# Selective-scan kernel: the order of softplus and side steps around a scan unit's B

## The chip, the cores and the metric

The kernel runs on one core of one Trainium2 chip, as one program. The metric is the device time of that core in microseconds (us); lower is better. The core has five engines that each work through their own instructions in order: TensorE (PE in the profile; PEld is its weight load), VectorE (DVE), ScalarE (ACT), GpSimd (POOL) and SyncE (SP, which here only issues DMA transfers).

## The reference

Four layers of a two-dimensional selective scan, each added to its input after a group norm. The sizes are a batch of 8, images of 48 x 48 (L = 2304 positions), 96 channels, 192 inner channels (Din), 16 states (N), 4 scan directions (K). The layers differ in small ways; layer 0 stands for them:

```python
xz = einsum('bhwc,ec->bhwe', x, in_proj_w);  xc, z = split(xz, 2, axis=-1)
xc = silu(depthwise_conv3x3(xc) + conv_b)
xs = stack([x0, x1, x0[..., ::-1], x1[..., ::-1]], axis=1)   # rows, columns, both ways
x_dbl = einsum('bkdl,kcd->bkcl', xs, x_proj_weight)
dts, Bs, Cs = split(x_dbl, [R, R + N], axis=2)
dts = einsum('bkrl,kdr->bkdl', dts, dt_projs_weight)
A = -exp(A_logs)
delta = softplus(dts + dt_projs_bias)
def step(h, inp):                       # along the L positions
    u, dl, Bv, Cv = inp
    dA = exp(dl[..., None] * A)
    h = h * dA + (dl * u)[..., None] * Bv[:, :, None, :]
    y = einsum('bkdn,bkn->bkd', h, Cv)
    return (h, y)
# ys + xs * Ds, the four directions summed, layer norm, * silu(z), out projection
```

For each channel and state there is one recurrence over the positions: h = h * dA + delta * u * B, and the output is the sum of h * C over the 16 states.

## The kernel before, in words

**Tiling.** Two images at a time make a pair (4 pairs a layer). The 192 channels of two images make three tiles `t` of 128 partitions. With two phases `ph` (row order or column order) and two directions `d` there are 12 groups for each layer and pair, and the 2304 positions of a group are cut into 3 chunks of 768. A chunk has 16 units `n`. One unit is one tensor of 128 partitions x 768 positions: two states of 64 channels each (`states`). A unit takes one scan instruction, so layers 0 to 2 have 3 layers x 4 pairs x 12 groups x 3 chunks x 16 = 6912 units. Layer 3 takes another, shorter path (class `Edge`, `l in short`), which the diff leaves as it is. Below, a block means the 16 units of one chunk.

**What one unit needs.** For unit n:

- B: the state's B row spread over 64 partitions. For ten units of a block, TensorE makes it in PSUM by four matmuls with the matrix `pick` (`spread`, L678); VectorE then multiplies it by delta * u (L810). For the six units n = 2, 5, 7, 10, 13, 15 (`pooled`) B comes from DRAM instead, by two DMAs from `xd` into `bb` (L740), and GpSimd makes the product with delta * u (`weigh`, L757). Then the PSUM buffer is used for the unit's decay.
- The decay exp(delta * a): one ScalarE activation (L780), into SBUF `da` or, for pooled units, into the PSUM buffer `b`.
- The scan, on VectorE (L814), and the product with C on GpSimd (`cb`, L823). C too is spread by DMA (L740).
- The sum over the states: TensorE adds the product into the PSUM accumulator `acc` (`add_up`, L870), two units later (`LAG = 2`).
- The last value of h is kept for the next chunk by a small ScalarE copy, the carry (`catch_up`, L698).

The PSUM pool of these buffers has two (`pb`, bufs=2): the B or decay of unit k + 1 takes the buffer of unit k - 1, which the scan of k - 1 frees.

**Softplus of the coming chunk.** `prepare` is a generator that makes delta and delta * u of the next chunk while the present one is scanned, in 15 steps; each `step(coming)` runs it to its next yield, one for each unit, beginning at n = 15 of the chunk before. For each half of 384 positions: the dt matmul (L614), then Abs, Relu and Exp on ScalarE (L622 to L624), then Ln, Identity and Identity (L626 to L628), then two steps of sums on TensorE, the first of `e` and `w1`, the second of `lg` and `x` (L634), then four copies to `dl` (L589), the product with u on VectorE (L642, L645), and four copies to `du`. In the text S1 to S15 are these steps: S1 at n = 15, S2 at n = 0, S3 at n = 1, first sums S4 at n = 2, second sums S5 at n = 3, S7 at n = 5, second half S8 at n = 6 to S15 at n = 13, its sums at n = 9 and 10.

**Side steps.** The work before a pair's scans (`prologue`: group norm, in projection L411 and L420, convolution L314, x projection L472) and after them (`epilogue`: L1031 to L1123) are generators as well. `side_step` advances one of them by one step. A step may issue work on any engine, DMAs on SP too.

**The order.** The instruction order of each engine is that of the Python loop in `run`, kept by `keep_order`. For unit k the loop issues: `collected()` (the copy of a finished accumulator, L887, when there is one), `get_ready(k + 1)` (loads for units k + 4 and k + 5, then B or decay of unit k + 1, then `weigh` and `decay` of unit k + 3), `catch_up()`, `scan(n)`, `add_up` of unit k - 2, and then `beside()`: one softplus step and one side step. At n = 3, where an accumulator was copied (`busy`), `beside()` stands ahead of `add_up`; at n = 2 (`ends`) there is no side step. So before, both kinds of step follow the B of unit k + 1 in the same pass.

Of the kernel before, what the change touches and what calls it, by code (L numbers as in the profile page):

```python
# [103 lines left out]
def ss2d_layers_kernel(ctx: ExitStack, tc: tile.TileContext, x_in, consts, weights, out):  # L104
# [470 lines left out]
    def load_dt(c):  # L575
        r = layers[c.l].rank
        c.dts = sm1.tile([64, SCAN], F32, name="dts", tag="dts")
        for b in c.batches:
            q0 = 32 * b if c.t == 2 else 0
            nc.sync.dma_start(  # L580
                c.dts[q0 : q0 + r, : c.m],
                state[c.l, c.p]["xd"][c.ph, b, c.d * r : (c.d + 1) * r, c.c0 : c.c0 + c.m],
            )
# [101 lines left out]
    def store_some(n):  # L685
        for _ in range(min(n, len(late_stores))):
            o, z, at = late_stores.pop(0)
            nc.sync.dma_start(o[:, at], z[:, at])

    def collected():  # L690
        some = bool(late_sums)
        while late_sums:
            late_sums.pop(0)()
        return some

    def catch_up():
        while late_act:
            nc.scalar.copy(*late_act.pop(0))  # L698
# [450 lines left out]
    def drain(g):  # L1149
        for _ in g:  # L1150
            pass

    def step(g):
        next(g, None)
# [7 lines left out]
    def side_step(*sides):  # L1162

        for s in sorted(sides, key=lambda s: (not s.held, s.made / s.total)):
            got = next(s.g, s)
            s.held = got is True
            if got is not s and got is not GATED:
                s.made += 1
                return True
        return False  # L1170
# [3 lines left out]
    def mark():  # L1174
        marks.append(len(tc._region_blocks()[0].instructions))
# [12 lines left out]
    LAG = 2  # L1188
    LOADS, DECAYS = 3, 2

    def run(pairs, short):


        def units():
            for l, p in pairs:
                for gi, (t, ph, d) in enumerate(groups):
                    if l in short:
                        c = Edge(l, p, t, ph, d)
                        for i in range(NS // QUAD):
                            yield (l, p, gi * (NS // QUAD) + i), c, i  # L1200
                        continue
                    group = {}
                    for i in range(len(SCANS)):
                        c = Chunk(l, p, t, ph, d, i, group, c if d == 1 and i == 0 else None)
                        for n in range(NS):
                            yield (l, p, (gi * len(SCANS) + i) * NS + n), c, n

        def begin(l, p, first=False):
            if l not in layers:
                layers[l] = Layer(l)  # L1210
            return prologue(l, p, l in short, first)

        todo = list(units())

        def rest_of_sum(k):
            before = todo[k - 1][1] if k > 0 else None
            if isinstance(before, Chunk) and (k == len(todo) or todo[k][1] is not before):
                before.add_up(NS)

        def get_ready(k):  # L1220

            def early(ahead, what):
                for i in range(0 if k == 0 else k + ahead, min(k + ahead + 1, len(todo))):
                    getattr(todo[i][1], what)(todo[i][2])

            early(LOADS + 1, "load_b")
            early(LOADS, "load")
            if k == 0:
                todo[0][1].decay(todo[0][2])
            if k < len(todo):  # L1230
                (l, p, _), c, n = todo[k]
                if n == 0 and c.first and l not in short:
                    c.group["carry"] = capool.tile([P, NS], F32, name="carry", tag="carry")
                c.spread(n)
            early(DECAYS, "weigh")
            for i in range(k + DECAYS if k else 1, min(k + DECAYS + 1, len(todo))):
                todo[i][1].decay(todo[i][2])

        rest = begin(*pairs[0], first=True)
        while next(rest) is not READY:  # L1240
            pass
        rest = Side(rest)
        chunks = list(dict.fromkeys(c for _, c, _ in todo))
        drain(prepare(chunks[0]))
        behind = ahead = Side()
        coming = iter(())
        done = None
        mark()
        get_ready(0)
        for k, ((l, p, unit), c, n) in enumerate(todo):  # L1250
            at = pairs.index((l, p))
            following = pairs[at + 1] if at + 1 < len(pairs) else None
            if l in short and unit == 0:
                mark()
            per = NS // QUAD if l in short else NS
            all_units = len(groups) * (per if l in short else len(SCANS) * per)
            place["tiles"] = 3 * unit // all_units
            store_some(1)
            if done:
                behind, done = Side(epilogue(*done), 199), None  # L1260
            if unit == LAG and following:
                ahead = Side(begin(*following), 311)
            if k == 0:
                coming_to = 1
                coming = prepare(chunks[coming_to])
            if n == max(0, per - 1 - DECAYS):
                while coming_to < len(chunks) and not chunks[coming_to].ready:
                    next(coming)
            if n == 10 and coming_to + 1 < len(chunks):
                z = chunks[coming_to + 1]  # L1270
                if (z.l, z.p) == (l, p):
                    load_dt(z)
            busy = collected()
            get_ready(k + 1)
            catch_up()
            c.scan(n)
            if n == per - 1:
                drain(coming)
                if unit + 1 + per == all_units:
                    drain(behind.g)  # L1280
                    drain(ahead.g)
                coming_to = chunks.index(c) + 2
                coming = prepare(chunks[coming_to]) if coming_to < len(chunks) else iter(())


            def beside():
                step(coming)

                for _ in range(10 if l in short else 0 if ends else 1):
                    side_step(rest) or side_step(behind, ahead)  # L1290

            ends = l not in short and k > LAG and todo[k - LAG][2] == 0
            if busy and l not in short:
                beside()
            if k >= LAG:
                (bl, bp, _), b, bn = todo[k - LAG]
                rest_of_sum(k - LAG)
                if bl in short:
                    collected()
                b.add_up(bn)  # L1300
                if k > LAG and todo[k - LAG - 1][0][:2] != (bl, bp):
                    done = todo[k - LAG - 1][0][:2]
            if not (busy and l not in short):
                beside()
        for i in range(len(todo) - LAG, len(todo)):
            collected()
            rest_of_sum(i)
            todo[i][1].add_up(todo[i][2])
            catch_up()
        collected()  # L1310
        rest_of_sum(len(todo))
        collected()
        drain(epilogue(*pairs[-1]))

    last = NLAYER - 1
    run([(l, p) for l in range(NLAYER) for p in range(NPAIR)], (last,))

    keep_order(*marks[:2])
# [8 lines left out]
    with tc.If(nc.values_load(again, min_val=0, max_val=1) > 0):  # L1327
        run([(last, p) for p in range(NPAIR)], ())
# [95 lines left out]
```

## Time and profile before

| | |
|---|---|
| median of 3 runs | 20188.83 us (20176.15 to 20194.05) |
| the profiled execution | 20200.44 us |
| its span, first to last instruction | 20198.6 us |
| mean granted TensorE clock | 0.908 |
| units of layers 0 to 2 (first scan's start to last scan's end) | 178 to 18298 us |
| DMA | 4200.80 MB, mean 208 GB/s |

In the lines of the page's groups, the parts are: line, engine, operation, tile written and tiles read with their shapes, count; then busy time in us and mean ns of one; then the idle time of the engine just before these instructions, and what ended most of it. A line of waits reads: engine and line that waited, what it waited for, total us, times, longest. A line of the timeline reads: start in us, duration, engine, line, operation, tiles, count. A line of windows reads: the stretch in us, its length, then the busy time and the number of instructions of PE, PEld, DVE, ACT and POOL, then the granted TensorE clock, the share of DMA time, GB/s. The busy time of TensorE is modelled, and its matmuls overlap.

### The profile page before, as it was taken

How to read it: one execution, taken by the hardware profiler on the slowest of the kernel's cores; microseconds unless marked ns; L12 is line 12 of the kernel's file. 1: busy time of each engine (PE TensorE's matmuls, PEld its weight loads, DVE VectorE, ACT ScalarE, POOL GpSimd, SP SyncE). 2: the span in 40 equal slices, each digit the busy share in tenths (PEclk: the TensorE clock that was granted, in tenths of full speed). 3: DMA queues.
4: the chain of work that ended last, by engine and by line, in shares of the span. 5: the costliest groups of instructions: out<-in, count | busy, mean ns of one | idle time of the engine just before them, and what ended most of it. 6: DMA issues, size and time to landing. Idle time of an engine off the chain costs nothing.

```text
span 20198.6 us, 314848 instructions
## 1 busy us (share of the span) xinstructions
PE 16790.8 (83%) x92962; PEld 7792.6 (39%) x92962; DVE 17667.0 (87%) x14161; ACT 16224.6 (80%) x30014; POOL 17769.4 (88%) x10121
## 2 busy tenths in 40 slices
PE   7888887887888888888887888888888887888886
PEld 3333333333333333333333333333333333334565
DVE  6999998998999999999999999999999999996553
ACT  6777887887887887887887887877877887887786
POOL 6999999999999999999999999999999999995442
PEclk9998998998998998998998999998999998999997
DMA  5888888888888888888888888888888888884221
GB/s 157 231 224 223 226 222 221 227 223 220 225 226 224 224 231 224 223 228 223 225 228 223 223 225 226 223 226 221 221 224 222 222 225 221 220 222 117 79 74 50
DMA packets 2021150, 4200.80 MB, mean 208 GB/s; under 512 B 375920, under 2 KB 789360, under 8 KB 2017904
## 3 DMA queue, kind: packets, MB, share of 16 engines
q1 hardware_dynamic: 2019440, 4180.55, 79.2%
q8 instruction: 762, 12.48, 0.3%
q14 instruction: 948, 7.77, 0.2%
HBM read 4026.64 MB, written 152.27 MB: 207 GB/s over the span
## 4 chain that ended last, share of the span: by engine, by line
PE 21%; ACT 17%; DVE 14%; DMA 10%; issue 9%; POOL 3%; SPq 2%; DVEq 0%; POOLq 0%; ACTq 0%
DVE da L814 7%; PE acc L870 5%; PE ps L634 4%; DMA bb<-xd 4%; DVE b L810 4%; DMA cb<-xd 4%; ACT b L780 3%; ACT dl L589 3%; PE ps L314 2%; PE b L678 2%; ACT du L589 2%; POOL cb L823 2%; DVE bb L814 2%; ACT da L780 2%; SPq L740 1%
## 5 line engine op out<-in xcount | busy, mean ns | idle before, releaser
L823 POOL TENSOR_TENSOR cb<-cb,da 128x768 f32<-128x768 f32 x4320 | 7835.9, 1819 | 749.3 <-issue 253.1
L870 PE MATMUL acc<-cb,twin 128*64 128x384 f32 x27648 | 7200.8, 539 | 721.3 <-POOL cb L823 704.5
L814 DVE TENSOR_TENSOR_SCAN da<-da,carry,b 128x768 f32<-128x768 f32 x2880 | 5223.2, 1814 | 176.0 <-DVE b L810 0.9
L757 POOL TENSOR_TENSOR bb<-bb,du 128x768 f32<-128x768 f32 x2592 | 4716.9, 1820 | 222.2 <-DMA bb<-xd 125.6
L823 POOL TENSOR_TENSOR cb<-cb,bb 128x768 f32<-128x768 f32 x2592 | 4706.8, 1816 | 100.2 <-DVE bb L814 50.7
L810 DVE TENSOR_TENSOR b<-du,b 128x768 f32<-128x768 f32 x4320 | 4085.6, 946 | 690.2 <-PE b L678 604.2
L678 PE MATMUL b<-brow,pick 96*64 96x512 bf16 (+2 forms) x18816 | 2852.5, 353 | 1886.2 <-DVE da L814 1528.4
L780 ACT ACTIVATE da<-dl,a 128x768 f32<-128x768 f32 x4320 | 4011.3, 930 | 213.5 <-POOL cb L823 183.0
L870 PEld LDWEIGHTS acc<-cb,twin 128*64 128x64 f32 x27648 | 2452.5, 149 | 2998.4 <-POOL cb L823 1333.5
L814 DVE TENSOR_TENSOR_SCAN bb<-b,carry,bb 128x768 f32<-128x768 f32 x1728 | 3109.6, 1800 | 106.0 <-ACT b L780 35.6
L780 ACT ACTIVATE b<-dl,a 128x768 f32<-128x768 f32 x2592 | 2335.3, 901 | 623.2 <-DVE da L814 598.4
L678 PEld LDWEIGHTS <-pick 96*64 96x64 bf16 x18816 | 1077.9, 115 | 4164.4 <-DVE da L814 2717.6
L814 DVE TENSOR_TENSOR_SCAN da<-da,b 128x768 f32<-128x768 f32 x1440 | 2525.3, 1754 | 87.4 <-DVE b L810 1.4
L314 PE MATMUL ps<-pad,diag 128*64 128x480 f32 (+1 forms) x8640 | 2339.7, 567 | 34.6 <-ACT du L589 24.4
L589 ACT COPY dl<-ps 64x384 f32<-64x384 f32 x3456 | 1632.6, 472 | 697.9 <-PE ps L634 659.6
L589 ACT COPY du<-ps 64x384 f32<-64x384 f32 x3456 | 1633.5, 473 | 200.7 <-DVE ps L645 109.8
L634 PE MATMUL ps<-du,cst 128*64 128x384 f32 (+1 forms) x7296 | 1704.5, 506 | 76.5 <-ACT du L628 65.6
L814 DVE TENSOR_TENSOR_SCAN bb<-b,bb 128x768 f32<-128x768 f32 x864 | 1502.1, 1739 | 145.5 <-ACT b L780 92.2
L634 PE MATMUL ps<-dl,cst 128*64 128x384 f32 (+1 forms) x7296 | 1485.2, 483 | 0.0
L614 PE MATMUL ps<-dts,w 6*128 6x384 f32 (+5 forms) x2432 | 961.4, 605 | 205.0 <-DMA dts<-xd 105.4
L622 ACT ACTIVATE du<-ps,w 128x384 f32<-128x384 f32 (+1 forms) x912 | 519.9, 570 | 714.6 <-PE ps L614 701.0
L314 PEld LDWEIGHTS ps<-pad,diag 128*64 128x64 f32 x8640 | 751.8, 139 | 885.0 <-issue 729.6
(144 smaller groups left out, 19166.4 us busy)
## 6 DMA issues: line engine op xcount, KB each, us to landing
cb<-xd SPq DMA_DIRECT2D x13952, 192.0 KB
bb<-xd SPq DMA_DIRECT2D x5184, 192.0 KB
brow<-xb SPq DMA_DIRECT2D x864, 72.0 KB
ey<-yd SPq DMA_DIRECT2D x256, 216.0 KB
cb<-xd SPq DMA_DIRECT2D x128, 384.0 KB
yd<-y SPq DMA_DIRECT2D x216, 192.0 KB
ex<-xs SPq DMA_DIRECT2D x256, 108.0 KB
xb<-parts SPq DMA_DIRECT2D x96, 216.0 KB
```

Source lines behind the costliest of these rows:

```text
L314: nc.tensor.matmul(ps[half, :m], ly.diag[:, int(t == 2), j, half], pad[:, r0 + dy : r0 + dy + nr, dx : dx + W], start=(j == 0), stop=(j == 8),
L589: nc.scalar.copy(z[64 * h : 64 * h + 64, g, at], v[64 * g : 64 * g + 64])
L614: nc.tensor.matmul(o[:, :m], ly.dtw[q0 : q0 + r, k, chans], dts[q0 : q0 + r, at], start=True, stop=True,)
L622: nc.scalar.activation(e, v, AF.Abs, bias=bias)
L634: nc.tensor.matmul(v[half], ident[:, half], z1, start=(i == 0), stop=(i == 3))
L678: nc.tensor.matmul(o[64 * h : 64 * h + 64], pick[:, b, n : n + 1].to_broadcast([2 * NR, 64]), rows, start=True, stop=True,)
L757: nc.gpsimd.tensor_mul(b, b, self.du[n % 2])
L780: nc.scalar.activation(da, self.dl[n % 2], AF.Exp, scale=layers[self.l].a2[:, int(self.t == 2), n % 2, k, i : i + 1],)
L810: nc.vector.tensor_mul(b, self.du[n % 2], b)
L814: nc.vector.tensor_tensor_scan(way(h), way(da), way(b), start, ALU.mult, ALU.add)
L823: nc.gpsimd.tensor_mul(c, c, h)
L870: nc.tensor.matmul(self.acc[64 * g : 64 * g + 64, a, : self.m // 2], twin, c[:, a, :], start=False, stop=(pair + 2 == NS and not self.turns),)
```

## The change

For pooled units of layers 0 to 2 (`ahead_of_b`), the softplus step and the side step are issued ahead of `get_ready(k + 1)`, so ahead of the next unit's B, and no `beside()` follows. At n = 15 the side step goes ahead; the first step of the next `prepare` goes right after the old one is drained, ahead of `add_up`. Units 3, 9 and 10 (`full`) have no side step any more. Units 1, 12 and 14 (`free`), whose next unit is pooled, have a second one, ahead of `add_up`. A block has 15 side steps before and after.

```diff
+    full, free = (3, 9, 10), (1, 12, 14)
...
+            def aside():
+                side_step(rest) or side_step(behind, ahead)
+
             busy = collected()
+            ends = l not in short and k > LAG and todo[k - LAG][2] == 0
+
+            ahead_of_b = l not in short and c.pooled(n)
+            if ahead_of_b:
+                if n < per - 1:
+                    step(coming)
+                if not ends and n not in full:
+                    aside()
             get_ready(k + 1)
             catch_up()
             c.scan(n)
@@
                 coming = prepare(chunks[coming_to]) if coming_to < len(chunks) else iter(())
 
+                if ahead_of_b:
+                    step(coming)
 
             def beside():
                 step(coming)
 
-                for _ in range(10 if l in short else 0 if ends else 1):
-                    side_step(rest) or side_step(behind, ahead)
-
-            ends = l not in short and k > LAG and todo[k - LAG][2] == 0
+                for _ in range(10 if l in short else 0 if ends or n in full else 1):
+                    aside()
+
+            if l not in short and n in free:
+                aside()
             if busy and l not in short:
                 beside()
...
-            if not (busy and l not in short):
+            if not (busy and l not in short) and not ahead_of_b:
                 beside()
```

## The prediction, made before the changed kernel ran

> **What bounds the kernel now.** I read the page's engine lines first, then its costliest groups, then the list of waits, then one block of 16 units in the timeline.
>
> ```profile
> PE 16790.8 (83%) x92962; PEld 7792.6 (39%) x92962; DVE 17667.0 (87%) x14161; ACT 16224.6 (80%) x30014; POOL 17769.4 (88%) x10121
> ...
> L823 POOL TENSOR_TENSOR cb<-cb,da 128x768 f32<-128x768 f32 x4320 | 7835.9, 1819 | 749.3 <-issue 253.1
> ...
> L814 DVE TENSOR_TENSOR_SCAN da<-da,carry,b 128x768 f32<-128x768 f32 x2880 | 5223.2, 1814 | 176.0 <-DVE b L810 0.9
> ...
> L810 DVE TENSOR_TENSOR b<-du,b 128x768 f32<-128x768 f32 x4320 | 4085.6, 946 | 690.2 <-PE b L678 604.2
> ```
>
> No engine is full. The units of layers 0 to 2 run from 178 to 18298 us: 432 blocks (6912 scans / 16) of 41.95 us each. In that stretch VectorE is busy 16756.6 us (38.8 a block), GpSimd 17055.7 (39.5). By the instruction records, GpSimd starts a unit's product 0.4 to 2.5 us after its scan ended and is back near the low end after units 1, 6, 9 and 14: it follows, VectorE leads. So **a block lasts as long as VectorE's work plus VectorE's waits** (3.2 us), and I price the change there.
>
> ```profile
> PEld L678 <- DVE da L814: 2717.6, 1691, 6.7
> PE b L678 <- DVE da L814: 1528.4, 1125, 6.1
> ...
> ACT dl L589 <- PE ps L634: 659.6, 411, 4.7
> DVE b L810 <- PE b L678: 604.2, 623, 10.5
> ...
> PEld ps L634 <- ACT du L628: 138.8, 166, 4.4
> ```
>
> Columns: total us, times, longest. TensorE stands at the next B (L678) until the scan two units earlier frees its PSUM buffer, mostly ahead of B(0), B(14) and B(8) (1.3, 1.1 and 0.5 us a block, sorted by unit). Yet VectorE waits for B elsewhere: at unit 1 (0.58 us a block), 11 (0.39), 6 and 12 (0.12 each). The last line matters below: the softplus sums wait for ScalarE's L628. One block (scan(0) begins at 10654.17), five answers: two of clock and busy time by window, then ScalarE, TensorE and VectorE.
>
> ```profile
> 10650.00:10655.00 5.00, 3.31 (x14) 0.97 (x16) 4.96 (x4) 2.44 (x6) 4.98 (x4) 0.76 1.03 239
> 10655.00:10660.00 5.00, 5.00 (x20) 2.20 (x22) 4.89 (x4) 4.91 (x10) 5.00 (x4) 0.56 1.00 241
> ```
> ```profile
> 10656.37 0.91 ACT L780 ACTIVATE b<-dl,a 128x768 f32<-128x768 f32 x1
> 10657.20 0.93 ACT L780 ACTIVATE da<-dl,a 128x768 f32<-128x768 f32 x1
> 10658.02 0.18 ACT L698 COPY carry<-da 128x1 f32<-128x1 f32 x1
> 10658.10 0.62 ACT L626 ACTIVATE dl<-du,ones 128x384 f32<-128x384 f32 x1
> 10658.62 0.60 ACT L627 ACTIVATE du<-du,ones 128x384 f32<-128x384 f32 x1
> 10659.26 0.62 ACT L628 ACTIVATE du<-du,ones 128x384 f32<-128x384 f32 x1
> ```
> ```profile
> 10658.82 0.85 PE L678 MATMUL b<-brow,pick 96*64 96x512 bf16 x4
> 10659.43 0.88 PE L870 MATMUL acc<-cb,twin 128*64 128x384 f32 x4
> 10660.08 1.52 PE L634 MATMUL ps<-du,cst 128*64 128x384 f32 x8
> ```
> ```profile
> 10658.68 1.79 DVE L814 TENSOR_TENSOR_SCAN bb<-b,carry,bb 128x768 f32<-128x768 f32 x1
> 10660.39 0.94 DVE L810 TENSOR_TENSOR b<-du,b 128x768 f32<-128x768 f32 x1
> ```
>
> TensorE's clock (0.76, 0.56) falls where it had stood before B(0). B(3) is made at 10658.82, well ahead of mul(3) at 10660.39; the sums come after it, at 10660.08, just after L628 ends at 10659.88. The change turns these two round.
>
> **What the Trainium skill says.** "TensorE: Matmul & The Clock Gate", Part 1: TensorE falls to half clock after an idle window of about 3.4 us and returns after a busy one. The trace agrees: 579 half-clock stretches, the shortest 3.4 us; in the blocks 18% of the time is at half clock, but 66% of unit 0's and 1% of that of units 4 and 5. Mul(1) waits 1.00 us where the clock is half and 0.05 where it is full. The same page's table says the queues of ScalarE, VectorE and GpSimd are strict FIFO; so here, what stands behind a waiting instruction waits too, and on TensorE as well the matmuls behind L870 stand while it waits 704.5 us for GpSimd.
>
> **The change part by part** (us a block, to be multiplied by 432).
>
> Counts: 15 side steps before and after; softplus step order unchanged. No operation is added or removed.
>
> 1. *Side steps at 14 (two) and ahead of B(0) at 15.* TensorE stands 1.77 us ahead of B(0); two more side steps there cost about 0.7 each (0.81 for a convolution step's four matmuls, none for a pure ScalarE step), so they fit. What stood between B(0) and B(1) shrinks from sum(13), L614 and a side step to sum(13) and L614, and the clock should stay up. Of the 0.58 at mul(1), about 0.25 are 27 blocks where L614 waits some 4 us for a late dt row (pair boundaries); those stay. **Gain 0.33** (0.1 to 0.45). B(0) had 1.0 of slack: cost 0; without that slack, each microsecond lands on mul(0).
>
> 2. *First sums ahead of B(3), at unit 2.* The longest new wait. TensorE cannot pass the sums before L628. Over all blocks L628 ends 3.48 after the exponential of b(2) starts, fixed within 0.05; that one needs the end of scan(0) (its PSUM buffer) and now starts 0.83 after it. With L614 ahead of sum(13), I take 0.35. Add the side step now ahead of L626 at unit 1 (estimate 0.2 of ScalarE: its 34.1 busy us a block less exponentials, softplus and copies leaves 2 to 3 for 15 side steps), the four matmuls left after L628 (half of eight in 1.3: 0.65), B(3) (0.05 + 0.55). Mul(3) can start 0.35 + 3.48 + 0.2 + 0.65 + 0.6 = 5.3 after scan(0). VectorE is there at 5.22 (measured) - 0.33 = 4.9. Wait 0.4; with scatter **loss 0.5** (0.2 to 0.9). Queued behind B(3): sum(16), B(4), the second sums; none is late, since B(4) has 1.2 of slack and VectorE moves later with it.
>
> 3. *Units 9 and 10: side steps out, second sums of half two ahead of B(11).* Sum(7) waits for GpSimd's product 7; the first sums start 0.24 after it, then a side step, then B(11). The side step (mean 0.43 between sums and B) becomes 1.3 of sums. Replacing one by the other in each block raises the wait from 0.39 to 0.80; blocks that had an L472 side step there (about as long as the sums) show 0.73, those with L314 0.27. I take **loss 0.3** (0 to 0.5). B(12) then has only sum(8) ahead: **gain 0.12**.
>
> 4. *Unit 5, 7, 13: softplus step and side step ahead of B(6), B(8), B(14).* S7, S9, S15 are ScalarE's, nothing on TensorE. A side step ahead of B(8) uses the 0.5 it stands; B(14) has 1.75 of slack: 0. B(6)'s 0.12 wait and the 0.22 of scan(10) for its exponential shrink: **gain 0.1** (0 to 0.2).
>
> 5. *Side steps closer together.* An epilogue's VectorE product (L1086, L1108; 32 a pair, 0.9 a block) follows ScalarE's step at once. Before, a scan always lay between; now none does at the second steps of 1, 12, 14 nor at 5, 7, 13, 15: 7 of 15 places, each 0.3 to 1.5 us of VectorE standing. 0.9 x 7/15 x 0.7 = 0.3, a part behind waits 2 and 3: **loss 0.1** (0 to 0.3).
>
> 6. *DMAs and GpSimd's own side work.* On SP the side steps' transfers now stand ahead of the cb and bb loads of their unit; one waiting for its copy holds these. Loads run 3 to 4 units (8 to 10 us) ahead, and GpSimd's longest group waits only 125.6 us in the run for bb: 0. Without that cover the delay would show at L757. GpSimd's products of the prologue only change places: 0. The unrolled last layer (18298 to the end) is untouched.
>
> Sum: -0.33 + 0.5 + 0.3 - 0.12 - 0.1 + 0.1 = +0.35 a block, x 432 = +151 us. The profiled execution took 20200.4 (span 20198.6 and 1.8 around), 11.6 over the median 20188.8. 20200.4 + 151 - 12 = **20340**.
>
> **The rivals.**
>
> - *Main case, slower:* mul(3)'s wait takes the place of mul(1)'s and mul(11)'s grows: 20340, own range 20240 to 20480. For: L628's time is fixed. Against: part 2 turns on 0.4 us. Chance 0.42.
> - *Faster: the clock stays up.* The two longest stands of TensorE are filled, half clock goes nearly everywhere; parts 1, 3b and 4 give 0.55, units 0 and 8 (waits 0.45 and 0.35 when cold, 42% and 24% of blocks) another 0.15; loss 2 only 0.2, 3 and 5 nothing: -0.5 x 432 = -216, 19973. It decides if mul(3) waits under 0.2 and mul(11) no more than now. For: 1.00 against 0.05 at mul(1). Against: the mean wait of VectorE for B is only 604 us in all. Chance 0.36.
> - *The two cancel,* 20190: waits 2 and 3 at 0.3 and 0.15. Chance 0.10.
> - *Clearly slower:* 2, 3 and 5 at their upper ends: 0.9 + 0.5 + 0.3 - 0.55 = +1.15, +497, about 20685. Chance 0.12.
> - That the change does not take effect is out: in the order of the built programs L634 stands ahead of L678 at unit 2 and a side step ahead of B(0).
>
> **How the numbers follow.** Faster 0.36, slower 0.42 + 0.12 = 0.54, within 0.2% (40 us, about what a measurement of this kernel can tell from no change; its runs lie within 18 us) 0.10. The range leaves out about a tenth at each end: from 19880, past the faster rival by as much as its own terms may be off (0.2 a block, 90 us), to 20680, just short of the worst.
>
> **What would show it.** Right: the wait of L810 for L678 at unit 1 falls under 0.3 us a block and one of about 0.5 appears at unit 3; "PE ps L634 <- ACT du L628" grows several times over; L678's wait for L814 falls by over a third; the mean clock rises above 0.93. Wrong: mul(3) starts with its scan as now, or the wait at mul(11) does not grow; then the faster case holds.

## The result, and the profile after

The changed kernel takes 20951.75 us (median of 5 runs, 20949.28 to 20959.5) against 20194.05 us for the kernel before (5 runs beside it): ratio 1.0378, 95% interval 1.0363 to 1.0392. It is **slower by 758 us**, or 1.75 us for each of the 432 blocks. The forecast was slower as well, but by 151 us; the measured time lies above the whole range (to 20680).

The page of the changed kernel: the span and the engines, then the groups that answer to those shown of before.

```profile
span 20949.9 us, 315270 instructions
...
PE 16850.4 (80%) x92962; PEld 7727.8 (37%) x92962; DVE 17722.3 (85%) x14161; ACT 16191.4 (77%) x30014; POOL 17790.5 (85%) x10121
...
L823 POOL TENSOR_TENSOR cb<-cb,da 128x768 f32<-128x768 f32 x4320 | 7833.6, 1817 | 1442.9 <-issue 388.5
...
L814 DVE TENSOR_TENSOR_SCAN da<-da,carry,b 128x768 f32<-128x768 f32 x2880 | 5223.8, 1814 | 174.6 <-ACT b L780 1.8
L810 DVE TENSOR_TENSOR b<-du,b 128x768 f32<-128x768 f32 x4320 | 4091.1, 947 | 1237.7 <-PE b L678 1007.8
```

No instruction was added, and the large groups take as long as before (1817, 1814 and 947 ns each, before 1819, 1814 and 946). What grew is idle time: ahead of VectorE's product with B (L810) from 690.2 to 1237.7 us, ahead of GpSimd's product (L823) from 749.3 to 1442.9. The list of waits says who made VectorE wait (columns: total us, times, longest us).

```profile
PEld L678 <- DVE da L814: 1713.7, 1087, 5.0
...
DVE b L810 <- PE b L678: 1007.8, 835, 11.2
PE b L678 <- DVE da L814: 983.9, 721, 4.3
...
PEld ps L634 <- ACT du L628: 594.0, 412, 8.0
...
PE ps L634 <- ACT du L628: 335.3, 264, 7.3
...
ACT dl L589 <- PE ps L634: 226.6, 230, 3.5
DVE b L810 <- PE acc L870: 221.2, 197, 5.5
PEld ps L1031 <- ACT ey L1074: 209.1, 102, 4.3
DVE eyc L1108 <- ACT ps L270: 185.5, 92, 7.4
```

The lines of before for these waits that are not shown yet (the first of them is for experiment e10):

```profile
DVE bb L814 <- ACT b L780: 127.8, 75, 5.2
...
PEld ps L1031 <- ACT ey L1074: 89.2, 77, 3.0
...
DVE eyc L1108 <- ACT ps L270: 85.4, 73, 7.4
...
DVE b L810 <- PE acc L870: 76.0, 59, 4.8
...
PE ps L634 <- ACT du L628: 65.6, 53, 3.1
```

TensorE stands less ahead of B (1713.7 and 983.9 us where it was 2717.6 and 1528.4), as the change arranges, and ScalarE waits less for the sums. But TensorE stands more where it now waits for ScalarE, ahead of the second half of the first sums (594.0 and 335.3 us, before 138.8 and 65.6), and VectorE waits 1007.8 us for B where it waited 604.2. Nearly all of the further 221.2 us that the profile puts down to L870 (before 76.0) is at unit 11 too: there the matmuls of B(11) and of the sum after it run in between each other, and the same wait for B goes to one name or the other.

One block of the changed kernel shows it. First the chain of waits through its start (start in us, duration, what), then the timeline of VectorE there.

```profile
6721.50 0.91 ACT b L780
6722.40 0.86 ACT da L780
6723.26 0.08 ACT carry L698
6723.34 0.52 ACT dl L626
6723.86 0.52 ACT du L627
...
6724.40 0.62 ACT du L628
...
6725.07 0.87 PE ps L634 x4
6725.93 0.33 PE b L678 x4
```
```profile
6719.71 1.75 DVE L814 TENSOR_TENSOR_SCAN da<-da,b 128x768 f32<-128x768 f32 x1
...
6724.10 1.73 DVE L814 TENSOR_TENSOR_SCAN bb<-b,bb 128x768 f32<-128x768 f32 x1
6726.30 0.96 DVE L810 TENSOR_TENSOR b<-du,b 128x768 f32<-128x768 f32 x1 [0.47 <-PE b L678]
```

The first line of VectorE is scan(0), the second scan(2), the third mul(3). The exponential of b(2) starts just after scan(0) ends (6721.46). Everything after it is in order on ScalarE until L628; the four matmuls of w1 need L628; B(3) stands behind them in TensorE's queue. VectorE ended scan(2) at 6725.83 and waits 0.47 us. This is a block in which nothing else went wrong; the mean is higher.

Sorting the records by unit gives the time from the end of scan(n - 1) to the start of unit n's first own instruction on VectorE, in us, means over all blocks. It holds waits and VectorE's other work, such as the products of the epilogue; where a side step moves from one unit to another, up to 0.08 us a block of such work moves with it. Left out are units 5 and 13, which have the two products with u (0.91 to 1.02 and 0.57 to 0.67 in all kernels), and units 4 and 9 (between -0.08 and 0.06). A small negative number comes from records of VectorE that overlap. The last column is the mean length of a block. The kernels e1 to b3 are the experiments below.

```
unit                  0     1     2     3     6     7     8    10    11    12    14    15 | block
before             0.13  0.58  0.02  0.01  0.12  0.13  0.04  0.22  0.38  0.12 -0.06  0.07 | 41.94
changed            0.07  0.38  0.11  1.03  0.04  0.26  0.26  0.18  0.73 -0.03  0.06  0.43 | 43.71
e1 sums 2 after B  0.08  0.38  0.11  0.08  0.15  0.26  0.21  0.17  0.99 -0.03  0.06  0.44 | 43.19
e5 step 3 early    0.08  0.36  0.34  0.48  0.03  0.28  0.31  0.18  0.84 -0.03  0.06  0.43 | 43.56
e6 sums 10 after B 0.07  0.38  0.10  1.10  0.04  0.27  0.29  0.18  0.17 -0.02  0.10  0.45 | 43.35
e7 both after B    0.07  0.39  0.10  0.11  0.16  0.26  0.20  0.17  0.30 -0.02  0.11  0.45 | 42.65
e3 sides only      0.02  0.29  0.11  0.04  0.13  0.31  0.18  0.17  0.25 -0.02  0.08  0.51 | 42.39
e9 all ahead       0.07  0.25  0.04  0.05  0.31  0.48  0.09  0.21  0.75 -0.02 -0.05  0.31 | 42.89
e10 5, 7 ahead     0.12  0.54  0.01  0.02  0.29  0.48  0.14  0.20  0.41  0.10 -0.06  0.07 | 42.59
e4 15 ahead        0.08  0.26  0.01  0.02  0.16  0.12  0.03  0.22  0.41  0.11 -0.06  0.28 | 41.85
e8 free only       0.13  0.36  0.09  0.04  0.01  0.10  0.00  0.16  0.31 -0.02  0.07  0.20 | 41.72
b1 15 to 12        0.04  0.25  0.04  0.05  0.16  0.11  0.02  0.22  0.40  0.12 -0.01  0.22 | 41.90
b2 10, 15 to 12, 13 0.05 0.22  0.03 -0.00  0.13  0.12  0.02  0.22  0.44 -0.06  0.14  0.31 | 41.88
b3                 0.03  0.27  0.04  0.09  0.18  0.12  0.02  0.22  0.20  0.04 -0.01  0.21 | 41.70
```

From before to changed: +1.02 at unit 3, +0.36 at 15, +0.35 at 11, +0.22 at 8, +0.13 at 7, +0.12 at 14, against -0.20 at 1 and -0.15 at 12.

### The profile page after: what moved, and what is told of

Its sections match the earlier page's. It is cut to its first block, busy times and chain, and to the rows that moved or that the text cites. A ratio compares the mean times of both kernels' runs of the same rounds, so it can differ in the third digit from the quotient of the medians.

```text
span 20949.9 us, 315270 instructions
## 1 busy us (share of the span) xinstructions
PE 16850.4 (80%) x92962; PEld 7727.8 (37%) x92962; DVE 17722.3 (85%) x14161; ACT 16191.4 (77%) x30014; POOL 17790.5 (85%) x10121
## 4 chain that ended last, share of the span: by engine, by line
PE 21%; ACT 21%; DVE 16%; issue 8%; DMA 7%; POOL 2%; SPq 2%; DVEq 0%; POOLq 0%; ACTq 0%
DVE da L814 7%; PE ps L634 5%; DVE b L810 5%; PE acc L870 5%; DMA cb<-xd 5%; ACT b L780 4%; ACT da L780 4%; ACT du L589 3%; PE ps L314 2%; ACT dl L589 2%; PE b L678 2%; POOL cb L823 2%; DVE bb L814 2%; DMA bb<-xd 2%; SPq L740 1%
## 5 line engine op out<-in xcount | busy, mean ns | idle before, releaser
L823 POOL TENSOR_TENSOR cb<-cb,da 128x768 f32<-128x768 f32 x4320 | 7833.6, 1817 | 1442.9 <-issue 388.5
L870 PE MATMUL acc<-cb,twin 128*64 128x384 f32 x27648 | 7084.3, 548 | 532.9 <-POOL cb L823 523.8
L814 DVE TENSOR_TENSOR_SCAN da<-da,carry,b 128x768 f32<-128x768 f32 x2880 | 5223.8, 1814 | 174.6 <-ACT b L780 1.8
L810 DVE TENSOR_TENSOR b<-du,b 128x768 f32<-128x768 f32 x4320 | 4091.1, 947 | 1237.7 <-PE b L678 1007.8
L823 POOL TENSOR_TENSOR cb<-cb,bb 128x768 f32<-128x768 f32 x2592 | 4707.4, 1816 | 192.2 <-DVE bb L814 106.5
L757 POOL TENSOR_TENSOR bb<-bb,du 128x768 f32<-128x768 f32 x2592 | 4709.4, 1817 | 177.8 <-DMA bb<-xd 93.8
L678 PE MATMUL b<-brow,pick 96*64 96x512 bf16 (+2 forms) x18816 | 2852.3, 355 | 1448.9 <-DVE da L814 983.9
L870 PEld LDWEIGHTS acc<-cb,twin 128*64 128x64 f32 x27648 | 2354.8, 151 | 3039.6 <-issue 1531.9
L814 DVE TENSOR_TENSOR_SCAN bb<-b,carry,bb 128x768 f32<-128x768 f32 x1728 | 3112.0, 1801 | 149.9 <-POOL cb L823 54.0
L814 DVE TENSOR_TENSOR_SCAN da<-da,b 128x768 f32<-128x768 f32 x1440 | 2525.5, 1754 | 88.8 <-ACT carry L698 2.3
L678 PEld LDWEIGHTS <-pick 96*64 96x64 bf16 x18816 | 1177.6, 117 | 3505.8 <-DVE da L814 1713.7
L314 PE MATMUL ps<-pad,diag 128*64 128x480 f32 (+1 forms) x8640 | 2082.6, 569 | 162.9 <-DVE eyc L1086 59.2
L634 PE MATMUL ps<-du,cst 128*64 128x384 f32 (+1 forms) x7296 | 1846.5, 520 | 366.8 <-ACT du L628 335.3
L814 DVE TENSOR_TENSOR_SCAN bb<-b,bb 128x768 f32<-128x768 f32 x864 | 1504.4, 1741 | 129.5 <-ACT b L780 47.6
L634 PE MATMUL ps<-dl,cst 128*64 128x384 f32 (+1 forms) x7296 | 1571.0, 492 | 0.0
L614 PE MATMUL ps<-dts,w 6*128 6x384 f32 (+5 forms) x2432 | 888.6, 559 | 302.1 <-ACT du L589 103.8
L634 PEld LDWEIGHTS ps<-du,cst 128*64 128x64 f32 x7296 | 654.9, 147 | 1164.8 <-ACT du L628 594.0
```

Source lines behind the costliest of these rows:

```text
L314: nc.tensor.matmul(ps[half, :m], ly.diag[:, int(t == 2), j, half], pad[:, r0 + dy : r0 + dy + nr, dx : dx + W], start=(j == 0), stop=(j == 8),
L614: nc.tensor.matmul(o[:, :m], ly.dtw[q0 : q0 + r, k, chans], dts[q0 : q0 + r, at], start=True, stop=True,)
L634: nc.tensor.matmul(v[half], ident[:, half], z1, start=(i == 0), stop=(i == 3))
L678: nc.tensor.matmul(o[64 * h : 64 * h + 64], pick[:, b, n : n + 1].to_broadcast([2 * NR, 64]), rows, start=True, stop=True,)
L757: nc.gpsimd.tensor_mul(b, b, self.du[n % 2])
L810: nc.vector.tensor_mul(b, self.du[n % 2], b)
```

## The experiments

The experiments write the conditions of the loop as four lists; the changed kernel in this form has the same order in layers 0 to 2.

```diff
+    steps_ahead, sides_ahead = (2, 5, 7, 10, 13, 15), (2, 5, 7, 10, 13, 15)
...
-            ahead_of_b = l not in short and c.pooled(n)
+            step_ahead = l not in short and n in steps_ahead
+            side_ahead = l not in short and n in sides_ahead
```

`beside()` then makes the softplus step only if it was not ahead, and the side step likewise. All times are medians, each beside runs of the kernel before (medians 20206 to 20216 us); so differences between two experiments are good to some 20 us. The theory at the start was that of the forecast, with larger sums: the loss is mostly the softplus sums ahead of B(3) and B(11). The rival: the moved side steps.

### The two sums

**e1: the first sums after B(3) again.**

```diff
-    steps_ahead = (2, 5, 7, 10, 13, 15)
+    steps_ahead = (5, 7, 10, 13, 15)
```

> The changed kernel with one thing undone: at unit 2 the first sums (L634 of e and w1) stand after B(3) again; all else as changed. Theory A (B(3) behind the sums, which wait for L628): mul(3)'s wait of 1.03 us a block falls to about 0.05, so the time falls by some 0.9 to 1.05 us x 432 = 390 to 450 us, to about 20500 to 20560; 'PE ps L634 <- ACT du L628' (594 and 335 us) falls back to about 140 and 65. Rival B (the loss comes from side steps that stand too close together, and the wait only moves): the time stays above 20800, and VectorE waits at another unit in place of 3.

20735.13 us, ratio 1.0268 (1.0250 to 1.0285): 217 us less than the changed kernel, half of what was expected. The wait at unit 3 is gone (1.03 to 0.08 a block), but unit 11 rises from 0.73 to 0.99 and unit 6 from 0.04 to 0.15. So neither theory as stated: the sums do make the wait at 3, and part of it had been standing in for waits later in the block.

**e6: the second sums of half two after B(11) again.**

```diff
-    steps_ahead = (2, 5, 7, 10, 13, 15)
+    steps_ahead = (2, 5, 7, 13, 15)
```

> The changed kernel with the second sums of half two (unit 10) after B(11) again; the first sums stay ahead of B(3). Theory A (these sums themselves hold B(11)): the wait at unit 11 falls from 0.73 us a block to 0.3 to 0.4, as where all softplus steps were put back (0.25), and the time by about 0.35 x 432 = 150 us, to some 20800. Rival B (GpSimd's product 7, which the sum ahead of them waits for, decides): the wait at 11 stays within 0.1 and the time above 20900.

20800.46 us, ratio 1.0292 (1.0275 to 1.0309), 151 us less, as theory A said; the wait at 11 falls to 0.17, further than expected. The sums of unit 10 themselves hold B(11).

**e7: both.**

> Both sums after B again (units 2 and 10); the steps of units 5, 7, 13 and 15 stay ahead, side steps as changed. If the two waits were independent, the two single undoings would add up: about 217 + 150 = 370 us less than the changed kernel, 20585. Theory A (a wait at unit 3 gives GpSimd and TensorE time and so shortens the wait at 11; undoing one alone leaves part of it at the other): more than the sum, near the kernel with all softplus steps put back, 20340 to 20450. Rival B (the softplus steps of units 5, 7, 13 and 15 cost something as well): 20500 or more.

20497.85 us, ratio 1.0142 (1.0125 to 1.0159): 454 us less than the changed kernel, more than 217 + 151 = 368. The two waits replace each other in part, as theory A had it. It is still 115 us above e3, in which no softplus step is moved: the steps of units 5, 7, 13 and 15 cost about 0.26 us a block, so the time lands at rival B's edge as well. No run separates these four.

**e5: the third softplus step ahead of the exponential of b(2).** Its Ln and two Identity (L626 to L628) come early, so the first sums need not wait for L628; their own work stays ahead of B(3).

```diff
-    steps_ahead = (2, 5, 7, 10, 13, 15)
+    steps_ahead = (1, 2, 5, 7, 10, 13, 15)
```

> The changed kernel with the third softplus step (L626 to L628) moved ahead of the exponential of b(2) on ScalarE, at unit 1; the sums stay ahead of B(3). It tells a wait for L628 from the mere work of the sums (1.3 us) ahead of B(3). Theory A1 (the wait for L628): L628 ends some 2 us earlier, mul(3)'s wait falls from 1.03 to 0.3 or less, the time by 300 us or more, to under 20650. Rival A2 (the sums' own time on TensorE): mul(3)'s wait stays above 0.7 and the time above 20800. That the exponential of b(2) comes 1.8 us later can cost up to 0.2 at scan(2).

20908.72 us, ratio 1.0347 (1.0330 to 1.0364), only 43 us less. L628 now ends 1.44 us before scan(1) does, on the mean, and not 1.25 after it, and the wait at unit 3 falls from 1.03 to 0.48. Not all of this fall is gained: scan(2) waits 0.23 more for its exponential, which is now behind L628, so VectorE comes to mul(3) that much later. Mul(3) itself starts 5.81 us after scan(0) ends, where in the changed kernel it started 6.15 after. So between a third and a half of the wait of 1.03 was for L628; the rest stays when L628 is early, with the sums (and what is ahead of them) in the way of B(3). The expectation of 0.3 was too low. The time follows mul(3), not its wait, and unit 11 waits 0.11 more.

### The side steps

**e3: side steps as changed, no softplus step moved.**

```diff
-    steps_ahead = (2, 5, 7, 10, 13, 15)
+    steps_ahead = ()
```

> Only the side steps as in the changed kernel (ahead at 5, 7, 13, 15, none at 3, 9, 10, two at 1, 12, 14); all softplus steps as before. Theory A (the softplus sums cost the most, +1.0 at unit 3 and +0.35 at unit 11): most of the loss goes; what is left is side steps too close together (the periods of units 6, 7, 13 and 14 had grown by 0.85 together) less the gain at units 1 and 12 (0.35): +0.2 to +0.5 us a block, 20280 to 20410. Rival B (side steps are the main loss): 20600 or more. Rival C (the side steps alone are a gain, since TensorE's stands are filled): under 20150.

20383.46 us, ratio 1.0093 (1.0076 to 1.0110), within theory A's numbers: the side steps alone cost about 180 us. Unit 15 now takes 0.44 more, 7 and 8 together 0.32 more, against -0.29 at unit 1, -0.13 at 11, -0.14 at 12.

**e8: only the redistribution (none at 3, 9, 10; two at 1, 12, 14), nothing ahead of a B.**

```diff
-    steps_ahead, sides_ahead = (2, 5, 7, 10, 13, 15), (2, 5, 7, 10, 13, 15)
+    steps_ahead, sides_ahead = (), ()
```

> The kernel before with only the redistribution: no side step at units 3, 9, 10, two at 1, 12, 14; nothing stands ahead of a B. Theory A (leaving 9 and 10 free of side steps shortens the waits at 11 and 12, which were 0.38 and 0.12; the second steps cost VectorE some stands ahead of scan(2) and scan(15), 0.1 to 0.2): -0.1 to -0.35 us a block, 20050 to 20160 against 20200. Rival B (second steps in one unit are costly by themselves): 20250 or more.

20117.29 us, ratio 0.9958 (0.9942 to 0.9975): faster than before, as theory A said. This part of the change is a gain; putting side steps ahead of B turns it into e3's loss, 266 us more.

**e9: side steps ahead, none redistributed.** Its list held 10 as well, which the expectation forgot; with `full` empty, a side step stands ahead of B(11) too.

```diff
-    full, free = (3, 9, 10), (1, 12, 14)
-    steps_ahead = (2, 5, 7, 10, 13, 15)
+    full, free = (), ()
+    steps_ahead = ()
```

> The kernel before with the side steps of units 5, 7, 13 and 15 ahead of the next B, one in each unit as before, no second ones and none left out. It tells the cost of standing ahead from that of doubling. Theory A (the cost is VectorE's epilogue step waiting for ScalarE with no scan between, at 5, 7 and 15, and TensorE's side step holding B(8)): stands of VectorE ahead of L1108 and L1086 rise from 0.08 to about 0.3 us a block, unit 8's wait to 0.2, mul(1)'s falls by 0.3: 20200 to 20290. Rival B (doubling at 1, 12, 14 is what costs): 20180 or less, as with unit 15 alone.

20638.99 us, ratio 1.0215 (1.0198 to 1.0232), far above both expectations. Units 6 and 7 take 0.54 more than before together, unit 11 0.37 more (the forgotten side step), unit 15 0.24 more. Standing ahead is what costs, not doubling.

**e10: side steps of 5 and 7 alone ahead.**

```diff
-    full, free = (3, 9, 10), (1, 12, 14)
-    steps_ahead, sides_ahead = (2, 5, 7, 10, 13, 15), (2, 5, 7, 10, 13, 15)
+    full, free = (), ()
+    steps_ahead, sides_ahead = (), (5, 7)
```

> The kernel before with the side steps of units 5 and 7 alone ahead of B(6) and B(8). Theory A (these two hold B(6), and by ScalarE the exponential of b(7): units 5 to 7 had grown by 0.63 us a block where all six stood ahead): +0.5 to +0.7, 20420 to 20500. Rival B (that kernel's loss came from units 10 and 15: +0.37 at 11 and +0.24 at 15): 20300 or less.

20474.92 us, ratio 1.0131 (1.0107 to 1.0155): theory A, 266 us for two places. Its list of waits:

```profile
DVE b L810 <- PE b L678: 711.2, 699, 9.2
...
DVE bb L814 <- ACT b L780: 175.4, 123, 3.6
...
DVE eyc L1108 <- ACT ps L270: 107.2, 61, 7.4
```

Before, these were 604.2, 127.8 and 85.4 us. By unit: mul(6) waits for B 0.33 us a block (before 0.15), mul(8) 0.20 (0.04), scan(7) for its exponential 0.19 (0.08), and VectorE stands 0.1 more ahead of the epilogue's products. (These are waits alone; the +0.35 at unit 7 in the table also holds 0.07 of products that moved there from unit 8.) So here a side step ahead of B holds three engines: TensorE with B behind it, ScalarE with the exponential of a later unit behind it, VectorE with the scan behind it.

**e4: the side step of unit 15 alone ahead of B(0).**

```diff
-    full, free = (3, 9, 10), (1, 12, 14)
-    steps_ahead, sides_ahead = (2, 5, 7, 10, 13, 15), (2, 5, 7, 10, 13, 15)
+    full, free = (), ()
+    steps_ahead, sides_ahead = (), (15,)
```

> The kernel before with one thing changed: the side step of unit 15 stands ahead of B(0) and not after the sum of unit 13. Theory A: mul(1)'s wait falls from 0.58 to about 0.3 us a block (the rest is the late dt row), nothing else moves: -0.2 to -0.3 us x 432 = -90 to -130 us, 20060 to 20100. Rival (the epilogue's VectorE step then stands ahead of scan(15) and costs what it gains): 20150 to 20230.

20179.16 us, ratio 0.9986 (0.9977 to 0.9995). The wait at mul(1) falls from 0.58 to 0.26, as worked out, but unit 15 takes 0.21 more. Of this, 0.08 is the work of the epilogue's products, which moved here from unit 0; most of the rest is that such a product, which now stands ahead of scan(15), waits for ScalarE (VectorE's stands ahead of L1086 and L1108 in the blocks rise from 0.08 to 0.24 us a block). The rival is right in its mechanism; a small gain is left.

### Versions meant to be faster

**b1** moves the side step of unit 15 to unit 12, as a second one; **b2** those of 10 and 15 to 12 and 13; **b3** is b1 with the side step of unit 9 ahead of sum(7), where TensorE waits for GpSimd. The start of each is the order before (`steps_ahead`, `sides_ahead` empty).

```diff
-    full, free = (3, 9, 10), (1, 12, 14)
+    full, free = (15,), (12,)          # b1
+    full, free = (10, 15), (12, 13)    # b2
+    full, free = (9, 15), (9, 12)      # b3
```

> A version meant to beat the kernel before: its order, only the side step of unit 15 moved to unit 12 as a second one, so nothing of it stands between B(0) and B(1) nor ahead of scan(15). Theory A: mul(1) waits 0.58 to 0.28 us a block and unit 15 stays at 0.1: -0.25 to -0.3 x 432 = -110 to -130 us, 20060 to 20100. Rival B (the second step at 12 delays ScalarE's exponentials of b(13) and b(15) and takes it back): 20150 or more.

20179.54 us, ratio 0.9985 (0.9978 to 0.9992). Mul(1) falls to 0.25, but unit 15 rises to 0.22 although no side step of its own stands there: VectorE stands 0.08 ahead of L1108 (unit 14's step; before 0.00), 0.06 for the exponential of b(15) (before 0.03) and 0.07 where the records name a cb load (before 0.04). Mostly rival B.

> A version that should beat the kernel before: its order, but the side steps of units 10 and 15 are left out there and stand as second ones at units 12 and 13, where TensorE stands ahead of B(14) and B(0) and VectorE has a product or a scan between. Theory A: mul(1) waits 0.58 to 0.3, mul(12) 0.12 to 0, no stand of VectorE ahead of scan(15): -0.35 to -0.45 us a block, 20000 to 20050 against 20194. Rival B (the second steps delay ScalarE's exponentials of b(15) or VectorE's epilogue steps wait as elsewhere): 20150 to 20250.

20172.92 us, ratio 0.9981 (0.9974 to 0.9988): again the wait at 1 is shortened (0.22) and given back at 14 and 15 (+0.2 each).

> The version before it, and the side step of unit 9 ahead of sum(7), where TensorE stands waiting for GpSimd's product 7, and not between the first sums and B(11). Theory A: the wait at unit 11 falls from 0.38 to about 0.2 as well: -0.4 to -0.5 us a block in all, 19990 to 20040. Rival B (the side step waits for ScalarE there and holds sum(7) and the softplus sums): no better than the version without it, 20060 or more.

20068.73 us, ratio 0.9929 (0.9910 to 0.9947). It gains less than hoped over the start, but it is the best version measured: 0.71% faster than before, 883 us faster than the changed kernel. The wait at unit 11 falls from 0.40 in b1 to 0.20. Its list of waits:

```profile
PEld L678 <- DVE da L814: 2195.3, 1489, 6.7
PEld acc L870 <- POOL cb L823: 1436.4, 1140, 6.2
...
DVE b L810 <- PE b L678: 457.6, 473, 10.7
```

Against b1, from which it differs by this one side step, TensorE stands less for GpSimd ahead of its sums (1436.4 us, in b1 1536.2), so the side step fills a part of that stand, and VectorE waits less for B (457.6, in b1 521.6, before 604.2).

## Why the prediction was wrong in size

The direction was right, and for the reason given: a wait at mul(3) takes the place of the one at mul(1), the wait at mul(11) grows. The size was off fivefold. Four runs, put in a row, add the parts of the change one at a time, in us a block:

| run | adds | block | added | predicted |
|---|---|---|---|---|
| before | | 41.94 | | |
| e8 | side steps redistributed | 41.72 | -0.22 | |
| e3 | side steps of 5, 7, 13, 15 ahead of B | 42.39 | +0.67 | |
| e7 | softplus steps of 5, 7, 13, 15 ahead | 42.65 | +0.26 | -0.45 for these three |
| changed | the two sums ahead of B(3), B(11) | 43.71 | +1.06 | +0.8 |

The -0.45 is steps 1, 4, 5 and the gain at mul(12) of step 3; the +0.8 is step 2 and the loss of step 3. The kernel lost 1.42 more than was forecast: 0.26 of it came with the sums and 1.16 with the rest. The steps of the sum by unit:

| step | predicted | measured |
|---|---|---|
| 1, mul(1) | -0.33 | -0.20 at unit 1; -0.32 in e4 alone |
| 2, mul(3) | +0.5 | +1.02 |
| 3, mul(11) and mul(12) | +0.3 and -0.12 | +0.35 and -0.15 |
| 4, steps ahead at 5, 7, 13 | -0.1 | -0.08 at 6, but +0.13 at 7, +0.22 at 8, +0.12 at 14; in e10 alone +266 us, 0.65 a block |
| 5, VectorE's stands ahead of the epilogue's products | +0.1 | +0.35 (0.08 to 0.43), of which 0.11 is also in the +0.13 at unit 7 |

**Step 4 failed in sign, and it is the largest miss.** It took a side step's place on TensorE to be its own time of matmuls, set it against the 0.5 us that TensorE stands ahead of B(8), and put the gain at 0.1. The two side steps of units 5 and 7, moved alone in e10, cost 0.65 us a block. A side step enters three queues at once. Its part on TensorE often waits for ScalarE: in e10 TensorE stands 0.55 us a block inside side steps during units 5 to 7, before 0.09, most of it for ScalarE. And ScalarE's queue is nearly full there: before, it stood idle for 1.1 us in all during units 4 to 9, some 16 us. In the changed kernel the exponential of b(7) starts 1.52 us after its buffer is free, before 1.06, and mul(8) waits 0.32 us a block for B, before 0.04. B(14), which had 1.75 of slack by the prediction, makes mul(14) wait 0.13. The softplus steps were priced at nothing as well, and e7 against e3 shows 115 us for the four that it holds apart.

**Step 2 had the right chain, with a wait twice the forecast.** L628 was taken to end 4.03 us after scan(0); it ended 4.46 after it. The exponential of b(2) started 0.60 after scan(0) and not 0.35, and from its start to L628's end passed 3.86 and not 3.68: the side step put ahead of L626 took 0.38 of ScalarE, and at times waits there (a tenth of the blocks above 4.55). After L628 it took another 1.7 until mul(3), not 1.3. But part of this wait stands in for others: by e1 and e6 against e7, the step is worth 217 us when undone alone and 302 when added alone, 0.5 to 0.7 a block.

**Step 5** was put at the low end, on the argument that a part would hide behind waits 2 and 3. It did not: 0.20 of the stands are at unit 15, 0.11 at 7, where neither of those waits is.

**Step 1**: the clock did not stay up. The mean granted clock went from 0.908 to 0.899, not above 0.93, and the share of half clock in the blocks from 18% to 20%. At unit 0 it fell from 66% to 50%, as argued; at units 12, 13 and 14 it rose from 3, 15 and 15% to 14, 37 and 29%. TensorE stands less ahead of B and more ahead of the first sums and inside side steps (2.58 us a block, before 0.44).

Of the four signs named, two came out: L634's wait for L628 grew over fourfold, L678's wait for L814 fell by over a third. The wait at unit 1 missed its mark (0.38, not under 0.3), and the clock missed it altogether. That the changes of the table's twelve columns add up to the longer block follows from how they are taken, and does not show that VectorE leads; that GpSimd waits longer for VectorE's scans (304.4 us ahead of L823, before 140.4) fits it. One figure of the prediction does not agree with itself: TensorE's stand ahead of B(0), 1.3 us a block in one place and 1.77 in another, is about 1.5 by the records. Nothing in the sum hangs on it.

Steps 4 and 5 and part of 2 have one root: a moved step was priced by its busy time on one engine, where it is a chain over three. Which of the softplus steps of units 5, 7, 13 and 15 costs the 115 us stays open.

## What to carry to other kernels

Before moving a step ahead of a critical instruction to fill a stand, list every queue that it enters and what it waits for there; an idle stretch of an engine is room only for work whose inputs are ready by then. Here a side step moved into a wait for another engine gained (b3's ahead of sum(7): unit 11 from 0.40 to 0.20), and work that ends a chain on a nearly full queue lost (the sums ahead of B(3)). And waits in one period replace each other: undoing one of two gave 217 and 151 us, both together 454.

## What was not expected of the hardware

The clock did not rise with the filling of TensorE's longest stands as a whole: 0.899 in the changed kernel, 0.918 where the same number of side steps was only redistributed (e8). Two experiments take this apart. With only the side step of unit 15 ahead of B(0), the clock rises (e4: 0.913 to 0.916 in all its runs, the kernel before beside it 0.903 to 0.909), and the share of half clock in unit 0 falls from 66% to 48%. With only those of units 5 and 7 ahead (e10), it falls to 0.898 in the profiled execution, and the share in the blocks is 20%, as in the changed kernel; in units 7 and 8 it goes from 24 and 16% to 36 and 22%. So moving these two side steps is enough for the lower clock. TensorE's waits inside side steps do not lower it by themselves: over a block they are 0.44 us before and 2.58 in the changed kernel, but 1.68 in e8, at the higher clock.

The prediction took the shortest half-clock stretch, 3.4 us, as agreement with a fall after an idle window. It is weak evidence, since stretches of both speeds come in steps of 3.41 us in these records. What TensorE did in the 3.41 us before says more. In the blocks of the kernel before, the clock fell 518 times, and in the step ahead of a fall TensorE was busy for 39% in the median (by its modelled records), and under 5% in only 4% of the cases. Ahead of the 3843 steps at full clock that followed another, it was busy for 77%. A limit at 44% parts the two with 194 misses among 4361; in the changed kernel one at 49% does so with 223 among 4420. So in this kernel TensorE need not stand idle for a whole step to lose its clock: being busy for less than about half of one was enough.
